# Four edits in a fused Mamba and mixture-of-experts kernel: the pieces of the first weight load, an undivided last block, further rows finished a block later, and the order of the gate's sums

## The chip, the cores and the metric

The kernel runs on one core of a Trainium2 chip. The metric is the device time of one execution in microseconds (us). The kernel before took 487.88 us, the median of three runs (486.55 to 489.39). One further execution was recorded by the hardware profiler; every duration below is from it.

A core has several engines that run their own instruction streams in order and wait for one another through semaphores. PE (TensorE) multiplies matrices and writes to PSUM banks; PEld is its loading of the stationary operand. DVE (VectorE), ACT (ScalarE) and POOL (GpSimd) work on tiles in SBUF and PSUM. SP (SyncE) mainly issues DMA transfers; POOL issues the indirect ones, which gather or scatter rows by a list of indices.

## The reference, cut to what matters

`x` holds 4096 tokens of width 256. A Mamba layer (inner width 512, 16 states, a convolution over 4 tokens) and a mixture of 8 experts (hidden width 1024, one expert for each token) follow each other, each with a residual sum and a layernorm. In short:

```python
xz = x @ W_in                                   # 256 -> 2 x 512
conv_in, gated = xz[..., :512], xz[..., 512:]
convolved = silu(depthwise_conv(conv_in, conv_w, 4 taps) + conv_b)
x_dbl = convolved @ W_x                         # delta, B (16), C (16)
delta = softplus(x_dbl[..., :1])
h_t = exp(delta * A) * h_(t-1) + delta * B * convolved[..., :16]
ssm_out = sum(h_t * C)                          # one number for each token
gated_out = (ssm_out + convolved * D_param) * silu(gated)
x1 = layernorm(x + gated_out @ W_out)
e = argmax(x1 @ Wr.T + br)                      # one expert for each token
out = layernorm(x1 + relu(x1 @ W1[e].T + b1[e]) @ W2[e].T + b2[e])
```

## The kernel before

**The Mamba layer** runs over 8 blocks of 512 tokens. The loop over k holds several blocks at once: block k is projected, block k-1 is gauged (`W_x`) and scanned, block k-2 passes the gate and the output projection, block k-3 is ranked for its experts. The channels lie on the 128 partitions, so the inner width of 512 is four column groups c = 0 to 3.

- `project` (L740 to L773) makes the products of `W_in` (L755), eight groups of 128 columns for each block: four for the convolution, four for the gate. Each needs two passes, since the 256 input columns are two times 128. In block 0 the first group alone is split into two halves of the tokens. ACT evicts each group (L760, L762, L764), and DVE adds the convolution's other three terms in `taps` (L736), which the text calls taps.
- `gauge` (L788), `scan` and `gate` (L868 to L885) follow. In the gate two products of TensorE, `py` at L873, write the state's sum for the first 256 tokens to one PSUM bank and for the second 256 to another. DVE then makes eight sums (L880): four column groups times two halves. The products with silu(gated) follow at L885, one for each group: those of groups 0, 1 and 2 on POOL, that of group 3 on DVE; in the last two blocks group 1 is on DVE too.
- `project_out` (L921 to L945) multiplies `sg`, the products' tile, by `W_out`: four steps j of 128 tokens, each over the four groups. It adds the residual, takes the layernorm's statistics and writes `x1` to memory (`x1d`). `choose` (from L948), `rank` (L975 to L1009) and `place` (L1020) work out each token's expert and place in the experts' lists; `table` and its `lookup` turn the counts into index tiles (`tidx` for rows, `widx` for weights).

**The experts** run as 32 blocks b of 128 rows, each with one expert's weights, in `blocks` (from L694). A block is cut into four quarters, which the main loop lays between the last Mamba blocks and runs in a row at the end:

- `prefetch` issues, up to two blocks ahead and on POOL, the gather of the rows (`xg`, L502) and that of the expert's weights (`we`, L520, three buffers).
- `scatter` (L661 to L663) writes the block before to `out`, on POOL.
- `turn` (L549, L551, L560) transposes the rows (`pg`), `hidden` makes the hidden layer: products at L577, the relu of the first half on ACT (L586), of the second on DVE (L588), both to `hT`.
- `close` (L590 to L645) multiplies `hT` by the second weights (L628) into the bank `pe`; `add_rows` makes the residual plus bias (L605). `finish` (L647 to L659) adds both to `r` (L650) and makes the layernorm (L251 to L262) with the result `y`.

Blocks 17, 20, 23, 26 and 29 (`LONG`) carry 32 or 64 **further rows** of the same expert besides their 128 (`ROOM`). Their products at L639 go to a bank `pf` of their own, and `finish` adds the bias to them (L656), sums the bank's parts (L658), makes a second layernorm and `scatter` a second DMA for them. All their tiles are slices of one buffer, called `long` in the trace. Block 31, the last, closes in two halves of the 256 output columns (L612): each half has eight products, its sum `r` (L621) and its statistics, so that the first half's sum can be made during the second half's products.

**What sets the order.** TensorE's instructions run in the order in which the program gives them (`manual_schedule` for PE alone). The order on DVE, ACT, POOL and SP is made by the planner of the tile framework, which may place an instruction elsewhere than its line stands. A bank (`ps.tile`, by tags `mm`, `tr` and `o`) or a buffer is handed on when its last reader is done.

**The start.** The loads are issued on two queues. SP loads the first half of each half of xT and `W_in` in pieces (`columns`), ACT loads the rest of xT:

```python
    for at in (slice(0, first), slice(first, TB)):
        nc.sync.dma_start(st[0]["xTb"][:, 0, at], xT[0:P, at])
        nc.scalar.dma_start(st[0]["xTb"][:, 1, at], xT[P : 2 * P, at])
        columns(slice(0, P) if at.start == 0 else slice(P, DI))
```

So `W_in` comes in pieces of 128, 384 and 512 columns, the first behind the first half of the tokens, the second behind the second half. The small loads `cw` and `cb` follow on ACT, and `wr` and the next blocks' loads on SP.

Of the kernel before, what the change touches and what calls it, by code (L numbers as in the profile page):

```python
# [37 lines left out]
F32 = mybir.dt.float32  # L38
# [61 lines left out]
def mamba_moe(  # L100
# [60 lines left out]
    for at in (slice(0, first), slice(first, TB)):  # L161
        nc.sync.dma_start(st[0]["xTb"][:, 0, at], xT[0:P, at])
        nc.scalar.dma_start(st[0]["xTb"][:, 1, at], xT[P : 2 * P, at])
        columns(slice(0, P) if at.start == 0 else slice(P, DI))
    cw = const.tile([P, CC, KC], F32, name="cw")
    nc.scalar.dma_start(cw, conv_w.rearrange("(c p) k -> p c k", p=P))
    cb = const.tile([P, CC], F32, name="cb")
# [80 lines left out]
        allow_small_or_imprecise_dtypes=True,  # L248
    )

    def layernorm(pool, rows, done, name, st=None):  # L251

        n = rows.shape[0]
        if st is None:
            st = pool.tile([P, 6], F32, tag="st", name=f"st{name}")[0:n, :]
            nc.vector.bn_stats(st, rows)
        mv = pool.tile([P, 2], F32, tag="mv", name=f"mv{name}")[0:n, :]
        nc.vector.bn_aggr(mv, st)  # L258
        sd = pool.tile([P, 1], F32, tag="sd", name=f"sd{name}")[0:n, :]
        nc.scalar.activation(sd, mv[:, 1:2], AF.Sqrt, bias=eps[0:n, :])  # L260
        nc.vector.reciprocal(sd, sd)
        nc.vector.tensor_scalar(done, rows, mv[:, 0:1], sd, ALU.subtract, ALU.mult)  # L262
# [232 lines left out]
    xgs, wes, turned, hid, last, open_, ys = {}, {}, {}, {}, {}, {}, {}  # L495


    xgf, openf, yf, ends_, wide_, xss, seldom_in, halves = {}, {}, {}, {}, {}, {}, [], []
    current = 0

    def gather(to, rows, at):
# [24 lines left out]
    def more_of(b):  # L526
        return ROOM[LONG[b]] if b in LONG else 0
# [64 lines left out]
    def close(b, half):  # L592
        we, hT = wes[b], hid[b]
        if half == 0:
            open_[b] = bank("o", f"pe{b}")
        py = open_[b]

        def out_weights(fc):
            return we[:, O2 + fc * D : O2 + (fc + 1) * D]

        def add_rows():
            xss[b] = m2.tile([P, D], F32, tag="xs", name=f"xs{b}")

            with tc.issue_after(last[b].ins):
                nc.vector.tensor_tensor(xss[b], xgs[b], we[:, OC : OC + D], ALU.add)  # L605

        if b == SURE - 1:


            at = slice(half * D // 2, (half + 1) * D // 2)  # L610
            for fc in range(FC):
                nc.tensor.matmul(  # L612
                    py[:, at], lhsT=hT[:, fc, :], rhs=out_weights(fc)[:, at],
                    start=(fc == 0), stop=(fc == FC - 1),
                )
            if half == 0:
                add_rows()
                halves.append(m2.tile([P, D], F32, tag="r", name=f"r{b}"))
                halves.append(a2.tile([P, 2, 6], F32, tag="sta", name=f"st{b}"))
            r, sts = halves  # L620
            nc.vector.tensor_tensor(r[:, at], py[:, at], xss[b][:, at], ALU.add)  # L621
            nc.vector.bn_stats(sts[:, half, :], r[:, at])
            if half == 1:
                ys[b] = m2.tile([P, D], F32, tag="y", name=f"y{b}")
                layernorm(m2, r, ys[b], f"m{b}", sts)
            return
        for fc in range(half * FC // 2, (half + 1) * FC // 2):
            nc.tensor.matmul(  # L628
                py[:, 0:D], lhsT=hT[:, fc, 0:P], rhs=out_weights(fc),
                start=(fc == 0), stop=(fc == FC - 1),  # L630
            )
        if half == 0:
            return
        if b in LONG:

            openf[b], n = bank("o", f"pf{b}"), more_of(b)
            for fc in range(FC):
                g = fc * n % P
                nc.tensor.matmul(  # L639
                    openf[b][g : g + n, 0:D], lhsT=hT[:, fc, P:], rhs=out_weights(fc),  # L640
                    start=(fc < P // n), stop=(fc >= FC - P // n), tile_position=(0, g),
                )
        add_rows()
        if b != SELDOM:
            finish(b)  # L645

    def finish(b):  # L647
        we, py, xs = wes[b], open_[b], xss[b]
        r = m2.tile([P, D], F32, tag="r", name=f"r{b}")
        nc.vector.tensor_tensor(r, py[:, 0:D], xs, ALU.add)  # L650
        ys[b] = m2.tile([P, D], F32, tag="y", name=f"y{b}")
        layernorm(m2, r, ys[b], f"m{b}")
        if b in LONG:
            m = more_of(b)
            xs, r, yf[b] = (ends_[b][0:m, n * D : (n + 1) * D] for n in (1, 2, 3))
            nc.vector.tensor_tensor(xs, xgf[b], we[0:m, OC : OC + D], ALU.add)  # L656
            for g in range(0, P, m):
                nc.vector.tensor_tensor(r, openf[b][g : g + m, 0:D], r if g else xs, ALU.add)  # L658
            layernorm(m2, r, yf[b], f"f{b}")  # L659

    def scatter(b):  # L661
        for rows, at in ((ys[b], index[b][1]), *(((yf[b], further[b][0 : more_of(b), :]),) if b in LONG else ())):
            moved = nc.gpsimd.indirect_dma_start(  # L663
                out=out, out_offset=bass.IndirectOffsetOnAxis(ap=at, axis=0),
                in_=rows, in_offset=None, bounds_check=T - 1, oob_is_err=False,
            )

            tc.declare_no_dep(moved.ins, group="rows", reason="blocks have no row in common")
            tc.add_to_no_dep_group("rows", moved.ins)
# [23 lines left out]
    def blocks():  # L693

        nonlocal current
        for b in range(SURE):
            current = b
            if b - 1 == SELDOM:
                seldom()
                finish(SELDOM)  # L700
            prefetch(b)

            if SELDOM - 6 <= b < SELDOM - 2:
                for n in range(SURE + b - SELDOM + 6, NSB, 4):
                    gather(seldom_rows()[:, (n - SURE) * D : (n - SURE + 1) * D], *index[n])

            if 0 < b:
                scatter(b - 1)
            for n in range(b + 2, NSB, 2) if b >= SURE - 2 else ():
                ys[n] = seldom_rows()[:, (n - SURE) * D : (n - SURE + 1) * D]  # L710
                scatter(n)
            if b not in turned:
                turn(b)
            hidden(b, 0)
            yield
            hidden(b, 1)
            yield
            if b + 1 in xgs and b + 1 < SURE:
                turn(b + 1)
            close(b, 0)  # L720
            yield
            close(b, 1)
            yield
# [9 lines left out]
    def taps(i, c):  # L733
        acc, xc = st[i]["acc", c], st[i]["xc"]
        for k in range(KC - 1):
            nc.vector.scalar_tensor_tensor(  # L736
                acc, xc[:, c, k : k + TB], cw[:, c, k : k + 1], acc, ALU.mult, ALU.add
            )

    def project(i, c):  # L740

        s = st[i]
# [5 lines left out]
            s["cv"] = a3.tile([P, CC, TB], F32, tag="cv", name=f"cv{i}")  # L748
            s["sg"] = a3.tile([P, CC, TB], F32, tag="sg", name=f"sg{i}")
        xc, cv, sg = s["xc"], s["cv"], s["sg"]  # L750
        pm = bank("mm", f"pm{i}_{c}")

        for at in (slice(0, first), slice(first, TB)) if i == c == 0 else (slice(0, TB),):
            for dc in range(DC):
                nc.tensor.matmul(  # L755
                    pm[:, at], lhsT=win[:, dc, c * P : (c + 1) * P], rhs=xTb[:, dc, at],
                    start=(dc == 0), stop=(dc == DC - 1),
                )
        if c >= CC:
            evicted = nc.scalar.activation(sg[:, c - CC, :], pm, AF.Silu)  # L760
        else:
            nc.scalar.copy(xc[:, c, KC - 1 :], pm)  # L762
            acc = a3.tile([P, TB], F32, tag="acc", name=f"acc{i}_{c}")
            evicted = nc.scalar.activation(  # L764
                acc, pm, AF.Identity, scale=cw[:, c, KC - 1 : KC], bias=cb[:, c : c + 1]
            )
            s["acc", c] = acc
            if c < CC - 1:
                taps(i, c)
# [96 lines left out]
    def gate(i):  # L866
        cv, sg = st[i]["cv"], st[i]["sg"]


        pys = [bank("o", f"py{i}_{g}") for g in range(2)]  # L870
        for g, py in enumerate(pys):
            at = slice(g * Q, g * Q + NS)
            nc.tensor.matmul(  # L873
                py[:, 0 : TB // 2], lhsT=ones[at, :], rhs=st[i]["hC"][at, :], start=True,
                stop=True, tile_position=(g * Q, 0),
            )
        for c in range(CC):
            for g, py in enumerate(pys):
                at = slice(g * TB // 2, (g + 1) * TB // 2)
                nc.vector.scalar_tensor_tensor(  # L880
                    cv[:, c, at], cv[:, c, at], dp[:, c : c + 1], py[:, 0 : TB // 2],
                    ALU.mult, ALU.add,
                )
            eng = nc.vector if c == CC - 1 or (c % 2 and i >= NB - 2) else nc.gpsimd
            eng.tensor_tensor(sg[:, c, :], cv[:, c, :], sg[:, c, :], ALU.mult)  # L885

# [321 lines left out]
```

## Time and profile before

| | |
|---|---|
| median of three runs | 487.88 us (486.55 to 489.39) |
| profiled execution | 486.12 us |
| its span, first to last instruction | 484.4 us |
| mean granted TensorE clock | 0.996 of full speed |
| moved by DMA | 89.65 MB, 185 GB/s |

The busy time of the engines in six stretches of the span shows where the work lies:

| us | stage | PE | DVE | ACT | POOL | GB/s |
|---|---|---|---|---|---|---|
| 0 to 10 | loads, first products | 8.1 | 1.3 | 2.8 | 3.3 | 219 |
| 10 to 40 | first two Mamba blocks | 29.3 | 19.3 | 23.9 | 0.7 | 88 |
| 40 to 170 | Mamba | 129.4 | 116.5 | 102.1 | 49.0 | 106 |
| 170 to 250 | Mamba and experts mixed | 79.2 | 66.8 | 47.5 | 31.7 | 158 |
| 250 to 400 | experts | 150.0 | 97.2 | 33.9 | 63.0 | 278 |
| 400 to 484.4 | experts, end | 75.3 | 39.3 | 13.8 | 38.2 | 197 |

How such lines are read. A busy-share line gives an engine, its busy us, the share of the span and the number of instructions. In a line of the waits the waiting engine, tile and line stand left of the arrow and the one that ended the wait right of it; then come the us in all, the number of waits and the mean. In a timeline a line has start, duration, engine, source line, operation, the tile written and the tiles read, and the shapes; "x16" says that so many like instructions are put together, and square brackets give the engine's idle time before and what ended it. Tile names leave out the block's number, and `pm`, `py`, `po`, `ph`, `pe`, `pf`, `pg` and `prx` are PSUM banks.

### The profile page before, as it was taken

To read this page: it belongs to the slowest core of one execution; us is meant where nothing else is said; L and a number is where in the kernel's file an instruction comes from. 1 tells how busy PE (TensorE), PEld (TensorE's weight loads), DVE (VectorE), ACT (ScalarE), POOL (GpSimd) and SP (SyncE) were. 2 spreads that over 40 slices of the span, in tenths; PEclk is the share of its full clock that TensorE was granted. 3 is DMA by queue.
4 is the path that set the end of the run, shared out by engine and by line. 5 is a ranking of instruction groups with operands and counts; after the bars stand their busy time and mean duration, and the time that the engine had idled before them with its cause. 6 is when DMAs were issued, how large, how long until landed. Compare 5 with 4: busy or idle time off the path is not lost. (4 is left out here: it accounts for less than half of the span.)

```text
span 484.4 us, 7580 instructions
## 1 busy us (share of the span) xinstructions
PE 471.3 (97%) x2618; PEld 352.9 (73%) x2618; DVE 340.3 (70%) x1117; ACT 224.0 (46%) x453; POOL 185.9 (38%) x194
## 2 busy tenths in 40 slices
PE   8999999999999999999999999999999999999984
PEld 5444555546464676777898999999989898889874
DVE  2587969798998997877799779445464645555343
ACT  3777768878878865848443132212111112122111
POOL 2001212444437454241514332535344456644621
PEclk9999999999999999999999999999999999999998
DMA  7501012130407918414677767999874399769700
GB/s 226 171 2 45 0 45 87 43 88 0 132 1 295 391 42 283 158 50 175 184 271 269 278 215 267 387 354 343 344 281 162 87 350 283 229 219 336 275 16 22
DMA packets 23049, 89.65 MB, mean 185 GB/s; under 512 B 4898, under 2 KB 14629, under 8 KB 19298
## 3 DMA queue, kind: packets, MB, share of 16 engines
q0 software_dynamic: 8672, 74.38, 42.2%
q1 hardware_dynamic: 13378, 14.50, 9.5%
q8 instruction: 21, 0.34, 0.3%
q10 hardware_dynamic: 960, 0.27, 0.3%
q14 instruction: 18, 0.15, 0.1%
HBM read 87.45 MB, written 9.54 MB: 200 GB/s over the span
## 5 line engine op out<-in xcount | busy, mean ns | idle before, releaser
L755 PE MATMUL pm<-xTb,win 128*128 128x512 f32 (+1 forms) x260 | 121.3, 597 | 0.2 <-DMA win<-in_W_in 0.2
L577 PEld LDWEIGHTS ph<-xgT,we 128*128 128x128 f32 x864 | 100.9, 192 | 6.3 <-issue 2.8
L577 PE MATMUL ph<-xgT,we 128*128 128x128 f32 x864 | 103.4, 276 | 0.6 <-issue 0.6
L628 PE MATMUL pe<-we,hT 128*128 128x256 f32 x416 | 96.1, 381 | 1.4 <-ACT hT L586 1.0
L628 PEld LDWEIGHTS pe<-we,hT 128*128 128x128 f32 x416 | 76.7, 190 | 11.9 <-ACT hT L586 1.2
L736 DVE SCALAR_TENSOR_TENSOR acc<-xc,cw,acc 128x512 f32<-128x512 f32 x96 | 72.9, 780 | 16.0 <-ACT acc L764 15.6
L755 PEld LDWEIGHTS pm<-xTb,win 128*128 128x128 f32 x260 | 47.6, 192 | 47.0 <-issue 40.9
L260 ACT ACTIVATE sdm<-mvm,eps 128x1 f32<-128x1 f32 x32 | 9.5, 296 | 143.7 <-DVE mvm L258 118.7
L520 POOL DMA_INDIRECT we<-in_experts,widx x32 | 33.7, 1054 | 90.5 <-DVE r L650 25.3
L921 PE MATMUL po<-wout,sg 128*128 128x264 f32 x256 | 64.1, 392 | 0.0
L885 POOL TENSOR_TENSOR sg<-cv,sg 128x512 f32<-128x512 f32 x22 | 32.8, 1495 | 59.3 <-DVE cv L880 45.9
L921 PEld LDWEIGHTS po<-wout,sg 128*128 128x128 f32 x256 | 46.1, 190 | 10.1 <-issue 2.9
L663 POOL DMA_INDIRECT out<-y,tidx x32 | 32.8, 1024 | 35.8 <-DVE y L262 23.4
L588 DVE TENSOR_SCALAR hT<-ph,we 128x128 f32<-128x128 f32 x108 | 31.4, 342 | 20.3 <-issue 8.8
L650 DVE TENSOR_TENSOR r<-pe,xs 128x256 f32<-128x256 f32 x31 | 13.1, 422 | 44.2 <-PE pe L628 37.7
L502 POOL DMA_INDIRECT xg<-x1d,tidx x32 | 32.1, 1004 | 31.0 <-DVE xd L811 7.5
L586 ACT ACTIVATE hT<-ph,we 128x128 f32<-128x128 f32 x108 | 30.7, 367 | 21.1 <-PE ph L577 14.3
L1009 POOL TENSOR_SCALAR rowh<-lrow,row,code 128x256 f16<-128x256 bf16 x20 | 26.0, 1308 | 27.2 <-DVE row L1001 26.0
L880 DVE SCALAR_TENSOR_TENSOR cv<-cv,dp,py 128x256 f32<-128x256 f32 x64 | 28.6, 471 | 3.4 <-PE py L873 3.4
L760 ACT ACTIVATE sg<-pm 128x512 f32<-128x512 f32 x32 | 19.0, 595 | 18.4 <-PE pm L755 16.0
L762 ACT COPY xc<-pm 128x512 f32<-128x512 f32 x32 | 18.6, 582 | 18.0 <-PE pm L755 17.8
L764 ACT ACTIVATE acc<-pm,cb,cw 128x512 f32<-128x512 f32 x32 | 25.1, 784 | 0.0
(224 smaller groups left out, 619.4 us busy)
## 6 DMA issues: line engine op xcount, KB each, us to landing
xb<-in_x SPq DMA_DIRECT2D x8, 512.0 KB, 6.2
x1d<-x SPq DMA_DIRECT2D x8, 512.0 KB, 6.0
xTb<-in_xT SPq DMA_DIRECT2D x7, 512.0 KB, 6.1
win<-in_W_in SPq DMA_DIRECT2D x1, 512.0 KB
we<-in_W_outT SPq DMA_DIRECT2D x1, 512.0 KB
wout<-in_W_out SPq DMA_DIRECT2D x1, 512.0 KB
we<-in_experts,widx POOLq DMA_INDIRECT x32
xg<-x1d,tidx POOLq DMA_INDIRECT x32
```

The costliest lines, as they stand in the source:

```text
L502: nc.gpsimd.indirect_dma_start(out=to, out_offset=None, in_=x1d[0:rows, :], in_offset=bass.IndirectOffsetOnAxis(ap=at, axis=0),)
L520: nc.gpsimd.indirect_dma_start(out=wes[n][:, :], out_offset=None, in_=experts, in_offset=bass.IndirectOffsetOnAxis(ap=weights[n], axis=0), ...
L577: nc.tensor.matmul(ph[:, n * w : (n + 1) * w], lhsT=we[:, at : at + P], rhs=xgT[:, dc * w : (dc + 1) * w], start=(dc == 0), stop=(dc == DC ...
L586: nc.scalar.activation(hT[:, fc, :], ph[:, n * w : (n + 1) * w], AF.Relu, bias=bias)
L588: last[b] = nc.vector.tensor_scalar(hT[:, fc, :], ph[:, n * w : (n + 1) * w], bias, 0.0, ALU.add, ALU.max)
L628: nc.tensor.matmul(py[:, 0:D], lhsT=hT[:, fc, 0:P], rhs=out_weights(fc), start=(fc == 0), stop=(fc == FC - 1),)
L663: moved = nc.gpsimd.indirect_dma_start(out=out, out_offset=bass.IndirectOffsetOnAxis(ap=at, axis=0), in_=rows, in_offset=None, bounds_chec ...
L736: nc.vector.scalar_tensor_tensor(acc, xc[:, c, k : k + TB], cw[:, c, k : k + 1], acc, ALU.mult, ALU.add)
L755: nc.tensor.matmul(pm[:, at], lhsT=win[:, dc, c * P : (c + 1) * P], rhs=xTb[:, dc, at], start=(dc == 0), stop=(dc == DC - 1),)
L880: nc.vector.scalar_tensor_tensor(cv[:, c, at], cv[:, c, at], dp[:, c : c + 1], py[:, 0 : TB // 2], ALU.mult, ALU.add,)
L885: eng.tensor_tensor(sg[:, c, :], cv[:, c, :], sg[:, c, :], ALU.mult)
L921: nc.tensor.matmul(po[:, 0 : D + NE], lhsT=sg[:, c, j * P : (j + 1) * P], rhs=wout[:, c, :], start=(c == 0), stop=(c == CC - 1),)
```

## The change

Four edits are made at once.

1. **First loads and products.** `W_in` comes in pieces of 128, 128, 256 and 512 columns; the second piece stands in front of the second half of xT. In block 0 the first two column groups are both split into halves of the tokens: TensorE makes group 0's first half, group 1's first half, group 0's second, group 1's second.
2. **The last block.** Block 31 closes like every other: eight products over all 256 columns, one sum, one set of statistics. `layernorm` loses its argument for statistics made before.
3. **Further rows.** Their bias is added in `close`; the bank's sums and the layernorm move into `finish_further`, which is called a block later, behind `hidden(b, 1)`. Their scatter comes a block later too, behind that of the next block's rows.
4. **The gate.** The sums of the first half (bank 0) are made for all four groups ahead of those of the second half, except for group 0, whose second sum stays second. The product of a group follows its second sum.

```diff
-        columns(slice(0, P) if at.start == 0 else slice(P, DI))
+        if at.start == 0:
+            columns(slice(0, P))
+            columns(slice(P, 2 * P))
+    columns(slice(2 * P, DI))
...
-    def layernorm(pool, rows, done, name, st=None):
+    def layernorm(pool, rows, done, name):
         n = rows.shape[0]
-        if st is None:
-            st = pool.tile([P, 6], F32, tag="st", name=f"st{name}")[0:n, :]
-            nc.vector.bn_stats(st, rows)
+        st = pool.tile([P, 6], F32, tag="st", name=f"st{name}")[0:n, :]
+        nc.vector.bn_stats(st, rows)
...
-        if b == SURE - 1:
-            at = slice(half * D // 2, (half + 1) * D // 2)
-            for fc in range(FC):
-                nc.tensor.matmul(
-                    py[:, at], lhsT=hT[:, fc, :], rhs=out_weights(fc)[:, at],
...
-            if half == 1:
-                ys[b] = m2.tile([P, D], F32, tag="y", name=f"y{b}")
-                layernorm(m2, r, ys[b], f"m{b}", sts)
-            return
...
-        add_rows()
+        xss[b] = m2.tile([P, D], F32, tag="xs", name=f"xs{b}")
+        with tc.issue_after(last[b].ins):
+            nc.vector.tensor_tensor(xss[b], xgs[b], we[:, OC : OC + D], ALU.add)
+        if b in LONG:
+            nc.vector.tensor_tensor(
+                ends_[b][0 : more_of(b), D : 2 * D], xgf[b], we[0 : more_of(b), OC : OC + D],
+                ALU.add,
+            )
         if b != SELDOM:
             finish(b)
...
+    def finish_further(b):
         if b in LONG:
             m = more_of(b)
             xs, r, yf[b] = (ends_[b][0:m, n * D : (n + 1) * D] for n in (1, 2, 3))
-            nc.vector.tensor_tensor(xs, xgf[b], we[0:m, OC : OC + D], ALU.add)
             for g in range(0, P, m):
                 nc.vector.tensor_tensor(r, openf[b][g : g + m, 0:D], r if g else xs, ALU.add)
             layernorm(m2, r, yf[b], f"f{b}")
...
             if 0 < b:
                 scatter(b - 1)
+                scatter(b - 2, False)
...
             hidden(b, 1)
+            finish_further(b - 1)
             yield
...
+        if i == 0 and c < 2:
+            if c == 0:
+                for n in range(2):
+                    products(n, slice(0, first))
+            products(c, slice(first, TB))
+        else:
+            products(c, slice(0, TB))
...
+        def skip(c, g):
+            at = slice(g * TB // 2, (g + 1) * TB // 2)
+            nc.vector.scalar_tensor_tensor(
+                cv[:, c, at], cv[:, c, at], dp[:, c : c + 1], pys[g][:, 0 : TB // 2],
+                ALU.mult, ALU.add,
+            )
+        skip(0, 0)
+        skip(0, 1)
+        for c in range(1, CC):
+            skip(c, 0)
         for c in range(CC):
-            for g, py in enumerate(pys):
-                at = slice(g * TB // 2, (g + 1) * TB // 2)
-                nc.vector.scalar_tensor_tensor(
-                    cv[:, c, at], cv[:, c, at], dp[:, c : c + 1], py[:, 0 : TB // 2],
-                    ALU.mult, ALU.add,
-                )
+            if c:
+                skip(c, 1)
             eng = nc.vector if c == CC - 1 or (c % 2 and i >= NB - 2) else nc.gpsimd
             eng.tensor_tensor(sg[:, c, :], cv[:, c, :], sg[:, c, :], ALU.mult)
```

More of the change, by code (lines that the diff above doesn't have):

```diff
@@ L495, in mamba_moe @@
     xgs, wes, turned, hid, last, open_, ys = {}, {}, {}, {}, {}, {}, {}
-    xgf, openf, yf, ends_, wide_, xss, seldom_in, halves = {}, {}, {}, {}, {}, {}, [], []
+    xgf, openf, yf, ends_, wide_, xss, seldom_in = {}, {}, {}, {}, {}, {}, []
     current = 0
@@ L599, in out_weights @@
             return we[:, O2 + fc * D : O2 + (fc + 1) * D]
[L601 to L605, printed above, removed]
-        if b == SURE - 1:
-            at = slice(half * D // 2, (half + 1) * D // 2)
-            for fc in range(FC):
-                nc.tensor.matmul(
-                    py[:, at], lhsT=hT[:, fc, :], rhs=out_weights(fc)[:, at],
-                    start=(fc == 0), stop=(fc == FC - 1),
-                )
-            if half == 0:
-                add_rows()
[L618 to L622, printed above, removed]
-            if half == 1:
-                ys[b] = m2.tile([P, D], F32, tag="y", name=f"y{b}")
-                layernorm(m2, r, ys[b], f"m{b}", sts)
-            return
         for fc in range(half * FC // 2, (half + 1) * FC // 2):
@@ L642, in close @@
                 )
-        add_rows()
+        xss[b] = m2.tile([P, D], F32, tag="xs", name=f"xs{b}")
[6 more added lines that the diff above has]
+            )
         if b != SELDOM:
@@ L659, in finish, with scatter @@
             layernorm(m2, r, yf[b], f"f{b}")
-    def scatter(b):
-        for rows, at in ((ys[b], index[b][1]), *(((yf[b], further[b][0 : more_of(b), :]),) if b in LONG else ())):
+    def scatter(b, main=True):
+        rows_at = ((ys[b], index[b][1]),) if main else ()
+        if not main and b in LONG:
+            rows_at = ((yf[b], further[b][0 : more_of(b), :]),)
+        for rows, at in rows_at:
             moved = nc.gpsimd.indirect_dma_start(
@@ L738, in taps @@
             )
+    banks = {}
     def project(i, c):
@@ L750, in project, with products @@
         xc, cv, sg = s["xc"], s["cv"], s["sg"]
-        pm = bank("mm", f"pm{i}_{c}")
-        for at in (slice(0, first), slice(first, TB)) if i == c == 0 else (slice(0, TB),):
+        def products(c, at):
+            if c not in banks:
+                banks[c] = bank("mm", f"pm{i}_{c}")
             for dc in range(DC):
                 nc.tensor.matmul(
-                    pm[:, at], lhsT=win[:, dc, c * P : (c + 1) * P], rhs=xTb[:, dc, at],
+                    banks[c][:, at], lhsT=win[:, dc, c * P : (c + 1) * P], rhs=xTb[:, dc, at],
                     start=(dc == 0), stop=(dc == DC - 1),
                 )
+        if i == 0 and c < 2:
[5 more added lines that the diff above has]
+            products(c, slice(0, TB))
+        pm = banks.pop(c)
         if c >= CC:
@@ L876, in gate @@
             )
-        for c in range(CC):
-            for g, py in enumerate(pys):
-                at = slice(g * TB // 2, (g + 1) * TB // 2)
-                nc.vector.scalar_tensor_tensor(
-                    cv[:, c, at], cv[:, c, at], dp[:, c : c + 1], py[:, 0 : TB // 2],
-                    ALU.mult, ALU.add,
-                )
+        def skip(c, g):
[8 more added lines that the diff above has]
+            skip(c, 0)
+        for c in range(CC):
+            if c:
+                skip(c, 1)
             eng = nc.vector if c == CC - 1 or (c % 2 and i >= NB - 2) else nc.gpsimd
```

## The prediction

> **What bounds the kernel now.** I read the page's busy shares first, then the table of TensorE's waits, then the stretches in order of time around the four edits.
>
> ```profile
> PE 471.3 (97%) x2618; PEld 352.9 (73%) x2618; DVE 340.3 (70%) x1117; ACT 224.0 (46%) x453; POOL 185.9 (38%) x194
> ```
>
> TensorE works from start to end. Its waits show how little could be won back:
>
> ```profile
> PE pe L628 <- ACT hT L586: 1.0, 1, 1.0
> ...
> PE pg L549 <- DMA xg<-x1d,tidx: 0.6, 1, 0.6
> ...
> PE prx L894 <- DVE rk L994: 0.4, 1, 0.4
> ...
> PE pe L612 <- DVE r L621: 0.4, 1, 0.4
> ```
>
> Apart from the time before the first product, no wait of TensorE is over 1.0 us, and none names a weight load, a bank held by the gate's sums, or the further rows' scatter. So an edit gains only where it takes away one of these few waits or shortens the two ends, and it loses wherever it makes one of TensorE's operands late. The tightest such operand is in the gate. This is the timeline in the gate of block 2 (start, duration, engine, line, tile; in brackets the idle time before it and what ended it):
>
> ```profile
> 102.25 0.47 DVE L880 SCALAR_TENSOR_TENSOR cv<-cv,dp,py 128x256 f32<-128x256 f32 x1
> ...
> 102.81 1.92 POOL L885 TENSOR_TENSOR sg<-cv,sg 128x512 f32<-128x512 f32 x1 [1.28 <-DVE cv L880]
> ...
> 104.54 2.23 PE L921 MATMUL po<-wout,sg 128*128 128x264 f32 x8
> 104.67 0.74 DVE L736 SCALAR_TENSOR_TENSOR acc<-xc,cw,acc 128x512 f32<-128x512 f32 x1
> 105.33 0.68 DVE L885 TENSOR_TENSOR sg<-cv,sg 128x512 f32<-128x512 f32 x1
> ...
> 106.06 0.30 PEld L921 LDWEIGHTS po<-wout,sg 128*128 128x128 f32 x2 [0.44 <-DVE sg L885]
> ```
>
> The output projection starts at 104.54 while the products of the gate are still being made: POOL's last ends at 104.73, DVE's at 106.01, and TensorE waits for the latter. Its eight passes are 0.22 apart, two for each of the four column groups, so the groups are wanted at 104.54, 104.98, 105.43 and 105.87.
>
> **The change part by part.** Edits without effect first. In the order in which the changed program issues its instructions, DVE and ACT take the **further rows** exactly where they did, in front of the next block's hT; the planner puts them back. Only four of the five further scatters move on POOL's queue, behind the next block's xg and weight gathers and its y (the fifth, of block 29, stays). Those gathers are issued some 0.9 us (one scatter) earlier, plus what POOL waited for the rows (6.7 us in three waits); TensorE waits for no weights, so this is 0, and a weight gather is never later. The **earlier release of the first PSUM bank** is 0 as well: no wait on it stands in the table. Both are hidden by slack that was there before.
>
> **The tail.** Now the last block closes in two column halves:
>
> ```profile
> 476.33 2.05 PE L612 MATMUL pe<-we,hT 128*128 128x128 f32 x16 [0.38 <-DVE r L621]
> ...
> 478.42 0.29 DVE L621 TENSOR_TENSOR r<-pe,xs 128x128 f32<-128x128 f32 x1 [1.81 <-PE pe L612]
> ...
> 479.85 0.41 DVE L262 TENSOR_SCALAR y<-r,mvm,sdm 128x256 f32<-128x256 f32 x1
> ```
>
> Products start at 474.00, y ends at 480.26: 6.26 us. The form it takes instead stands in block 30: products at 466.87, sum r at 470.63 (3.76 us), y ends at 472.70 (2.07 us more), together 5.83. The wider add and statistics (0.42 and 0.43 against 0.29 each) cost less than the wait between the halves, so **-0.43**; bounds 0 and -0.7.
>
> **The start.** The loads of W_in put a second 128-column piece in front of the second half of xT.
>
> ```profile
> 4.57 1.35 PEld L755 LDWEIGHTS pm<-xTb,win 128*128 128x128 f32 x4 [0.52 <-issue]
> 6.66 0.73 PEld L755 LDWEIGHTS pm<-xTb,win 128*128 128x128 f32 x4 [0.73 <-DMA xTb<-in_xT]
> 7.75 0.30 PEld L755 LDWEIGHTS pm<-xTb,win 128*128 128x128 f32 x2 [0.37 <-DMA win<-in_W_in]
> ```
>
> The first piece is unchanged, so products start at 4.57 and the first half ends at about 6.4. I take the new piece to land where the xT half did, 6.66; the second group's first half runs to 7.63. The xT half lands 128 KB later, at the 226 GB/s of the page's first slice 0.58 us, so about 7.24: in time. Two second halves of 0.86 bring the third group to 9.35, against 9.58 now (7.75 with four passes of 0.43 and a slow first one): **-0.2**. Bounds -0.35 (all idle gone) and +0.4 (xT as late as 8.2). SP's queue has one issue more (0.4 to 0.5 us) ahead of wr, the next xT and the rest; the router product that needs wr comes at 10.9, the others after 17. The first eviction moves from 7.82 to about 8.6, and with it DVE's taps; the cover is 4.6 us (block 0's last cv ends at 20.02, is read at 24.62).
>
> **The gate.** Here the edit costs. Of eight sums L880 two finish a column group. Before, group 1 was complete after the 4th sum, group 2 after the 6th, group 3 after the 8th; now all first halves come first, so groups 1, 2, 3 are complete after the 6th, 7th and 8th. The slots between the taps stay. POOL's product for group 1 thus moves from 99.70 to where that for group 2 was, and group 2's has to follow it directly. Do POOL and DVE disturb each other? The same form takes POOL 1.27 us beside sums and 1.92 beside a tap; and in the gate of block 1, where three products run back to back from 71.08 to 74.85, a tap took
>
> ```profile
> 73.59 1.81 DVE L736 SCALAR_TENSOR_TENSOR acc<-xc,cw,acc 128x512 f32<-128x512 f32 x1
> ```
>
> instead of 0.74. [...] Taken without it, 1.27 us for each product, group 2 would come in time and the gate would cost 0; with it: no product runs at 99.70, so DVE's L965 (0.78 there, 0.18 at 75.81) is free, and the 6th sum ends 0.60 earlier, at 102.12. Product 1 takes its row's 1.92: 102.21 to 104.13. Product 2 follows with 1.27: to 105.40, just as TensorE wants it. But the tap that ran free at 104.67 is now issued at 104.07 and held; as at 73.59 the next instruction follows 1.73 later (75.32), at 105.80, and that is product 3: to 106.48, with 0.05 for the signal 106.53, wanted at 105.87. TensorE loses 0.66 and 0.11 for a slow restart, 0.77 in place of today's 0.30 (0.19 and 0.11): **+0.5**.
>
> Gate of block 3 has the same times within 0.1: +0.5. It is followed by the wait for rk above (at 138.7), which could absorb that; but DVE runs gapless from 128 to 140 and is itself 0.47 later, so the wait ends later too and I absorb nothing. Gate of block 4: product 3 ends at 160.21 instead of 159.74, wanted at 160.05, loss 0.3; then DVE's lateness moves tidx (163.70), behind it POOL's gather of xg, and the wait of pg for xg ends 0.47 later: +0.5 for the pair. In the gates of blocks 0, 1, 5, 6 and 7 the last product comes ahead of its use by 1.6, 0.9, 7, 5 and 2 us; a hold of up to 1.2 us fits, save for a little in block 1. Sum of the gates **+1.5**; bounds +0.3 (waits after gates 3 and 4 absorb, the hold half as long) and +4.2 (1.4 each: product 2 starved behind tap and product 3, and DVE 1.3 late afterwards).
>
> **Sum.** +1.5 - 0.43 - 0.2 = +0.9 us. The profiled execution took 486.12 (span 484.4 and 1.7 around it), so 487.0; the runs' median is 487.88, 1.76 above it, and the same step gives **488.8**.
>
> **The rivals.**
>
> - *The gates pile up (slower).* Place: gates of blocks 2 to 4. If POOL's second product is passed over by the tap and by product 3 (0.66 + 0.61), group 2 comes at 106.7, a net loss of 1.13, and DVE is 1.27 late where rank and gather are waited for: 1.13 + 1.27 + 1.27 = 3.7, less 0.63: 491.0 or more. For: POOL's 1.92 shows that it can lose its turn. Against: at 72.31 and 73.58 it got it each time. It decides from 1.02 us lost per gate (3.07 together is 2.44 after the gains).
> - *The further rows' stall goes (faster).* In block 30 TensorE idles about 2.1 us, since
>
> ```profile
> 464.69 0.88 DVE L658 TENSOR_TENSOR long<-pf,long 64x256 f32<-64x256 f32 x2 [3.58 <-remote]
> ...
> 466.87 3.72 PE L628 MATMUL pe<-we,hT 128*128 128x256 f32 x16 [0.97 <-ACT hT L586]
> ```
>
>   hT stands on ACT behind the further rows' square root. Finishing them later would take that away: -2.1 - 0.63, without a gate loss 485.2. Against: the issue order of DVE and ACT has not changed there, so in this part the change doesn't do what it says.
> - *The gates are hidden (nothing but the ends).* The operands slip inside slack, -0.63: 487.25.
>
> **How the numbers follow.** Likeliest case 0.66 (486.8 to 490.2 by its bounds and the runs' own spread of 1.4 each way), pile-up 0.12, stall gone 0.06, hidden 0.16. 0.5% is 2.44 us, about what a measurement of this kernel can tell from no change: the lines are 485.4 and 490.3. Slower: the pile-up and a little of the likeliest case's upper end, 0.13. Faster: most of the stall's case, 0.05. Within: 0.82. The range 486.7 to 491.0 leaves out the stall case and the far ends.
>
> **What the profile after would show.** Start: three L755 weight loads' waits at 6.66 and 7.75 gone or under 0.2, third group near 9.35. Gates 2 to 4: POOL's three L885 as one early and two adjoining, a tap of 1.7 to 1.8 after them, the wait of po's load for sg at 0.8 to 0.9 instead of 0.44. Tail: 5.8 us from the last block's first product to the end of y. Wrong would be: a wait of TensorE on POOL's sg over 1 us, a wait on win over 0.5, or sdf behind hT on ACT.

## The result, and the profile after

The changed kernel takes **495.39 us** (median of four, 493.37 to 496.49) where the kernel before takes 488.29 beside it (486.55 to 489.39): a ratio of 1.0143, 95% interval 1.0100 to 1.0186, or 7.1 us slower. The forecast was 488.8 with a range up to 491.0. The profiled execution of the changed kernel took 494.83 us (span 493.1), 8.7 us above the profiled one of before.

When this was measured both kernels ran slower than in any later set: before alone stood at 488 there and at 483.9 to 484.6 in four later sets, in whose 187 executions it never passed 486.81; in three of those sets the change was measured again, and came out 0.9 to 1.7 us slower.

Where do the 8.7 us lie? Like instructions of TensorE were put beside each other in the two traces. They are 1.8 us late when block 0's router products begin (18.78 against 16.98), 5.0 late behind the gates of blocks 2 to 4 (183.93 against 178.91), 9.3 late in block 30 (474.84 against 465.51), and 8.7 at the end. So: start +1.8, gates +3.2, expert blocks +4.3, tail -0.6.

First the page's busy shares, then the waits of TensorE in the profile after (waiting engine and line, what ended the wait; us in all, number, and the longest single wait, not the mean as was said where the views were explained):

```profile
PE 475.4 (96%) x2606; PEld 355.0 (72%) x2606; DVE 344.3 (70%) x1115; ACT 223.5 (45%) x453; POOL 185.3 (38%) x194
```

```profile
PE pe L604 <- ACT hT L588: 3.2, 2, 2.3
PE po L933 <- DVE sg L897: 1.7, 3, 0.6
...
PE pm L749 <- DMA win<-in_W_in: 0.6, 1, 0.6
...
PE po L933 <- POOL sg L897: 0.6, 2, 0.3
```

All four are new or larger: `po` now waits for the gate's products in five places, the first products wait for `W_in`, and one wait for hT is 2.3 us long.

**The start** (timeline after, TensorE and its weight loads):

```profile
4.44 2.04 PE L749 MATMUL pm<-xTb,win 128*128 128x256 f32 x4
7.06 6.19 PE L749 MATMUL pm<-xTb,win 128*128 128x256 f32 x16 [0.58 <-DMA win<-in_W_in]
```

```profile
7.06 4.50 PEld L749 LDWEIGHTS pm<-xTb,win 128*128 128x128 f32 x14 [1.30 <-DMA win<-in_W_in]
```

The second piece lands at 7.06, 0.4 us later than I took it to. But this is the smaller part of the cost: the fourteen loads behind it take 4.50 us, and the passes of 256 columns follow each other by 0.43 us until 10.2, where before they had gone over to 0.22 by 7.0. TensorE stays at half rate.

**The gate of block 2** (timeline after, chosen lines of DVE, POOL and PEld):

```profile
103.39 0.47 DVE L883 SCALAR_TENSOR_TENSOR cv<-cv,dp,py 128x256 f32<-128x256 f32 x1
103.88 0.73 DVE L728 SCALAR_TENSOR_TENSOR acc<-xc,cw,acc 128x512 f32<-128x512 f32 x1
103.94 1.83 POOL L897 TENSOR_TENSOR sg<-cv,sg 128x512 f32<-128x512 f32 x1 [3.10 <-DVE cv L883]
104.54 1.28 DVE L981 TENSOR_TENSOR oh<-back,best 128x32 bf16<-128x32 f32 x1
105.74 0.47 DVE L883 SCALAR_TENSOR_TENSOR cv<-cv,dp,py 128x256 f32<-128x256 f32 x1
106.29 1.27 POOL L897 TENSOR_TENSOR sg<-cv,sg 128x512 f32<-128x512 f32 x1 [0.52 <-DVE cv L883]
106.64 0.94 DVE L984 TENSOR_TENSOR earlier<-earlier,here 128x8 bf16<-128x8 bf16 x1
107.61 0.30 PEld L933 LDWEIGHTS po<-wout,sg 128*128 128x128 f32 x2 [0.70 <-POOL sg L897]
108.17 0.68 DVE L897 TENSOR_TENSOR sg<-cv,sg 128x512 f32<-128x512 f32 x1
108.90 0.30 PEld L933 LDWEIGHTS po<-wout,sg 128*128 128x128 f32 x2 [0.99 <-DVE sg L897]
```

POOL's product for group 1 stands where the forecast put it (103.94 is 102.21 in the time of before, since all is 1.73 late here). What it holds is not a tap but `oh`, a small one-hot operation: 1.28 us, where before it took 0.18, although POOL's product for group 2 was running there (102.81, 1.92 us, shown in the prediction):

```profile
103.40 0.18 DVE L969 TENSOR_TENSOR oh<-back,best 128x32 bf16<-128x32 f32 x1
```

The seventh sum, queued behind it, starts 7.86 us after `py` instead of 7.35, group 2's product waits for that sum, and TensorE waits for both remaining products. Group 2's product in turn stands beside `earlier`, another small two-input operation (0.94 here, 0.34 before), and behind that in DVE's queue come a tap and the product for group 3.

**Block 25** (timeline after, then TensorE's granted clock in three stretches: start and end, length, busy us and instructions of PE, clock, DMA share, GB/s):

```profile
426.44 1.14 ACT L588 ACTIVATE hT<-ph,we 128x128 f32<-128x128 f32 x4 [4.44 <-remote]
426.56 1.13 DVE L590 TENSOR_SCALAR hT<-ph,we 128x128 f32<-128x128 f32 x4 [3.91 <-remote]
```

```profile
423.40:426.80 3.40, 1.12 (x8) 1.00 0.90 160
426.80:430.20 3.40, 3.33 (x8) 0.50 0.18 58
430.20:433.60 3.40, 3.40 (x20) 1.00 0.08 25
```

TensorE has finished the hidden layer's products at 423.8, but ACT and DVE, which wait for them alone, go on only at 426.4; "remote" means that the profile finds no releaser. TensorE stands for 2.3 us, and its next 3.4 us run at half rate: 2.3 and half of 3.4 make the 4.05 lost here. The trace of before has such a wait, of 3.58 us in block 30, which the forecast took for a stall of the kernel's own. The trace of after has it too, at the same place, beside the one in block 25:

```profile
473.92 0.88 DVE L644 TENSOR_TENSOR long<-pf,long 64x256 f32<-64x256 f32 x2 [3.62 <-remote]
```

In both traces TensorE stands in block 30 for 0.4 and 0.2 us with nothing named and then for 0.9 to 1.0 us for hT. None of the fourteen profiles taken later, of any kernel, has these waits.

**The tail**:

```profile
483.23 3.62 PE L604 MATMUL pe<-we,hT 128*128 128x256 f32 x16
...
486.88 0.42 DVE L635 TENSOR_TENSOR r<-pe,xs 128x256 f32<-128x256 f32 x1 [2.00 <-PE pe L604]
...
488.55 0.41 DVE L264 TENSOR_SCALAR y<-r,mvm,sdm 128x256 f32<-128x256 f32 x1
```

From the last block's first product to the end of y: 5.73 us, where it was 6.26.

### The profile page after: what moved, and what is told of

Same layout as the page of the kernel before. It is cut to its first block, busy times and chain, and to the rows that moved or that the text cites. A ratio compares the mean times of both kernels' runs of the same rounds, so it can differ in the third digit from the quotient of the medians.

```text
span 493.1 us, 7553 instructions
## 1 busy us (share of the span) xinstructions
PE 475.4 (96%) x2606; PEld 355.0 (72%) x2606; DVE 344.3 (70%) x1115; ACT 223.5 (45%) x453; POOL 185.3 (38%) x194
## 5 line engine op out<-in xcount | busy, mean ns | idle before, releaser
L749 PE MATMUL pm<-xTb,win 128*128 128x512 f32 (+1 forms) x264 | 122.7, 598 | 0.6 <-DMA win<-in_W_in 0.6
L604 PE MATMUL pe<-we,hT 128*128 128x256 f32 x432 | 101.2, 386 | 3.2 <-ACT hT L588 3.2
L604 PEld LDWEIGHTS pe<-we,hT 128*128 128x128 f32 x432 | 80.8, 193 | 14.5 <-ACT hT L588 3.6
L728 DVE SCALAR_TENSOR_TENSOR acc<-xc,cw,acc 128x512 f32<-128x512 f32 x96 | 71.7, 769 | 17.2 <-ACT acc L768 16.9
L749 PEld LDWEIGHTS pm<-xTb,win 128*128 128x128 f32 x264 | 49.6, 196 | 46.8 <-issue 39.8
L579 PE MATMUL ph<-wide,we 128*128 128x160 f32 (+1 forms) x160 | 24.6, 311 | 1.1 <-DVE r L635 0.7
```

The lines of the kernel that those rows point to most:

```text
L579: nc.tensor.matmul(ph[:, n * w : (n + 1) * w], lhsT=we[:, at : at + P], rhs=xgT[:, dc * w : (dc + 1) * w], start=(dc == 0), stop=(dc == DC ...
L604: nc.tensor.matmul(py[:, 0:D], lhsT=hT[:, fc, 0:P], rhs=out_weights(fc), start=(fc == 0), stop=(fc == FC - 1),)
L728: nc.vector.scalar_tensor_tensor(acc, xc[:, c, k : k + TB], cw[:, c, k : k + 1], acc, ALU.mult, ALU.add)
L749: nc.tensor.matmul(banks[c][:, at], lhsT=win[:, dc, c * P : (c + 1) * P], rhs=xTb[:, dc, at], start=(dc == 0), stop=(dc == DC - 1),)
```

## The experiments

Changes in us are the ratio's distance from 1 times the 484 us of before.

**Each edit alone.** Four kernels, each before with one edit.

The start: the loads and the order of the first products, as in the change's diff.

> Before with the first edit alone (four pieces of W_in, two split column groups). The clock theory: TensorE waits about 0.8 us for the second piece near 6.3 us, that wait keeps it at half rate until about 10.2 us, and the router product pw starts 1.8 us later than before (13.1 instead of 11.3): time +1.8 us, about 489.8. The rival, that the wait alone costs: full rate again from about 8 us, pw at most 0.6 us later, +0.6. A third, that the profiled execution was an accident of its loads: -0.2 to 0.

Measured: 482.74 against 484.29, ratio 0.9974 (0.9956 to 0.9991), -1.3 us. The clock theory's +1.8 did not come; nor did a loss of any size.

```profile
6.71 4.57 PE L760 MATMUL pm<-xTb,win 128*128 128x256 f32 x16 [0.26 <-DMA win<-in_W_in]
11.12 0.51 PE L474 MATMUL pw<-wr,ones 128*128 128x8 f32 x4
```

Here the piece lands at 6.71, the sixteen passes take 4.57 us instead of 6.19, and `pw` begins at 11.12. So the loss of 1.8 us is not in every execution of this edit. Nor does this profile show where the whole gain comes from: `pw` is only 0.17 ahead of before's 11.29.

The gate:

> Before with the fourth edit alone (all first halves of the gate's sums ahead). If the profile of the change is typical, TensorE waits twice in each of the gates of blocks 2 and 3 (0.45 and 0.74 beyond a pass) and once in block 4's, blocks 2 to 4 add 1.1, 1.1 and 1.0 us, in all +3.2 us: about 491.2. The forecast's own size, one wait of 0.66 in each, would give +1.5: 489.5.

Measured: 486.67 against 484.29, ratio 1.0049 (1.0031 to 1.0068), +2.4 us. That interval, +1.5 to +3.3, holds the 3.2 of the first profile and touches the forecast's 1.5; the profile decides. Its three gates are those of the change to 0.01 us: +1.11, +1.10 and +0.96 at the marks behind them. They are the same within 0.02 us in all five profiles with the changed gate.

The further rows, run in two sets:

> Before with the third edit alone (further rows finished and scattered a block later). The forecast's step says 0: DVE and ACT keep their order, only four scatters move on POOL's queue; block 25 shows no wait of TensorE above 0.7 us: about 488. The rival, that the move on POOL's queue makes the 4 us loss seen in block 25 of the changed kernel: +4 us, about 492, with ACT and DVE both idle for about 4 us ahead of hT in block 25.

> The third edit alone once more, beside the changed kernel. If the large loss comes from the further rows' place on POOL's queue, then whenever the changed kernel loses over 4 us this one does too. If not, it stays within 0.5 us of before. In both cases blocks 17, 20, 23 and 26 keep the order of DVE and ACT, and only POOL's scatter moves.

Measured: ratio 1.0004 (0.9990 to 1.0018) and 0.9996 (0.9981 to 1.0010). No wait on "remote" is in either profile. The forecast's 0 holds, to within the 0.9 us of the intervals.

The tail:

> Before with the second edit alone (last block undivided). The forecast's step says -0.43: 5.8 us from the last block's first product to the end of y, about 487.6. The rival, that the single block costs more than it saves (its sum has to wait for all products): 0 or up to +0.5.

Measured: 483.35 against 484.29, ratio 0.9988 (0.9969 to 1.0007), -0.6 us, and 5.73 us from the first product to the end of y. The interval holds 0 as well; the trace's -0.53 is the better number: the stretch is 5.73 in all six profiles with the undivided block, and 6.25 or 6.26 in all ten with the divided one.

**The change again**, three times, beside other kernels.

> The changed kernel as it is, once more. If the four edits add up as each did alone (-1.3, +2.4, +0.2, -0.6), it is 0.7 us slower than before; in the profile gates of blocks 2 to 4 as in the first profile (+3.2), and no 4 us loss in block 25. The rival, that the edits act together or that the loss in block 25 is theirs: 5 to 9 us slower again, with ACT and DVE idle for 4 us ahead of hT in block 25.

> The changed kernel a third time. By the sum of the single edits and its second measurement it is 1 to 2.5 us slower than before. The rival: where the first measurement's conditions return (before near 488, above the 484 of the later runs), it is 5 to 9 us slower, and the profile shows a loss of 2 us or more in one of the blocks 24 to 30, with DVE waiting for nothing that the program names.

> The changed kernel once more, for the loss in block 25 alone. If before stands near 484 again, the changed kernel is 1 to 2.5 us slower and shows no such loss; if before stands near 488, as in the first measurement, it should be 5 to 9 us slower and show a loss of 2 us or more in blocks 24 to 30. Anything else (before near 484 and the change over 4 us slower, or before near 488 and the change within 2.5) would tie the loss to the change or free it from it.

Measured: 485.25, 485.18 and 485.15; ratios 1.0036 (1.0018 to 1.0053), 1.0028 (1.0015 to 1.0042) and 1.0019 (1.0005 to 1.0033): +1.7, +1.4 and +0.9 us. The sum of the single edits is -1.3 + 2.4 + 0.2 - 0.6 = +0.7, a little under all three; each of its terms is itself uncertain by 0.7 to 0.9. The loss in block 25 is in none of these profiles, and before was near 484 each time: the first measurement's conditions did not come back, so whether that loss needs them and the change together is not told. The second profile shows the start with a wait as long as in the first:

```profile
6.93 2.89 PEld L749 LDWEIGHTS pm<-xTb,win 128*128 128x128 f32 x14 [1.27 <-DMA win<-in_W_in]
```

The same fourteen loads behind the same wait (1.27 and 1.30) take 2.89 us here and took 4.50. Between these two profiles the wait does not decide, the clock does: here the full rate had begun at 5.65, ahead of the wait.

**The start's wait made longer, and filled.** The late piece:

```diff
-        if at.start == 0:
-            columns(slice(0, P))
-            columns(slice(P, 2 * P))
+        columns(slice(0, P) if at.start == 0 else slice(P, 2 * P))
     columns(slice(2 * P, DI))
```

> The first edit alone, with its second piece of W_in moved back behind the second half of xT, so that TensorE always waits for it, about 1 us near 6.3. The clock theory: a wait of that length keeps the clock at half rate for another 3.4 us, to about 10.2; pw at 12.8 to 13.3 instead of 11.1, time +1.5 to +2 against before. The rival, that only the wait counts: full rate before 8 us, pw at 11.6, time +0.3.

Measured: 484.51 against 483.87, ratio 1.0000 (0.9982 to 1.0017); the medians' difference of 0.6 us lies within that interval. The edit missed its aim: in the profile the piece still lands at about 6.4, TensorE does not wait and `pw` stands at 10.96. So the clock theory of the start was not tested here. This profile loses 1.6 us elsewhere, at 44 us, which is read in the last section.

With the wait filled:

```diff
-                for n in range(2):
-                    products(n, slice(0, first))
+                products(0, slice(0, first))
+                for n in range(5):
+                    nc.tensor.transpose(idle[:, n % 4 * P : (n % 4 + 1) * P], ident, ident)
+                products(1, slice(0, first))
```

> As the one with the late piece, but five transposes of the identity (0.21 us each at half rate, results unused) fill TensorE's wait for that piece. The clock theory: the clock goes up as in the kernel before, by about 7 us, and pw stands at 11.3 to 11.7, 1 to 2 us earlier than with the empty wait, although TensorE has more to do and the same loads to wait for. The rival: the same time as the late piece without the transposes, or later by part of their 1.07 us.

Measured: 483.20, ratio 0.9978 (0.9966 to 0.9990), -1.1 us, though TensorE has more to do. One of its 20 executions lies above 484.2 us; of the late piece's 12 it is 8, all eight at a granted clock of 0.995 where the other four have 0.996 to 0.999. But `pw` at 11.36 is later than without the transposes, so the reason given in the expectation is not shown: since the late piece made no wait, this pair does not tell whether the transposes help at the start or by what comes later. This profile also shows something about the gate, which is before's own here. In block 2 TensorE waits 0.96 us for the product of group 3, because `oh` is held in the old order too:

```profile
103.47 1.30 DVE L985 TENSOR_TENSOR oh<-back,best 128x32 bf16<-128x32 f32 x1
```

**What in the gate costs.** The edit alone, with POOL's product for group 1 left out:

```diff
-            eng.tensor_tensor(sg[:, c, :], cv[:, c, :], sg[:, c, :], ALU.mult)
+            if c != 1 or i >= NB - 2:
+                eng.tensor_tensor(sg[:, c, :], cv[:, c, :], sg[:, c, :], ALU.mult)
```

> The fourth edit alone, and in the gates of blocks 0 to 5 POOL's product for column group 1 is left out (that group's sg stays silu(gated); outputs and the experts' lists differ, so only the gates of blocks 2 to 4 are read, not the whole time). The theory that POOL's product 1 holds DVE: the small one-hot operation that took 1.28 us there takes about 0.2, the seventh sum comes 1.1 us earlier than with the edit alone, TensorE's waits for sg in gates 2 and 3 shrink from 1.2 us to 0.2 at most. The rival, that the sums' new order alone makes the products late: the seventh sum within 0.3 us of its place with the edit alone, and waits of at least 0.5.

```profile
102.94 0.18 DVE L978 TENSOR_TENSOR oh<-back,best 128x32 bf16<-128x32 f32 x1
103.05 0.47 DVE L879 SCALAR_TENSOR_TENSOR cv<-cv,dp,py 128x256 f32<-128x256 f32 x1
...
103.60 1.27 POOL L894 TENSOR_TENSOR sg<-cv,sg 128x512 f32<-128x512 f32 x1 [4.35 <-DVE cv L879]
...
106.21 0.30 PEld L930 LDWEIGHTS po<-wout,sg 128*128 128x128 f32 x2 [0.45 <-DVE sg L894]
```

`oh` is back at 0.18, the seventh sum starts 6.75 us after `py` (7.86 with the edit, 7.35 before), the last wait is 0.45, and was 0.44 before. In the three gates TensorE loses nothing against before, although `earlier` is still held (0.94 or 0.95). With that product left out the new order of the sums is free; the product that meets `oh` is the cost.

The same product on DVE, nothing left out:

```diff
-            eng = nc.vector if c == CC - 1 or (c % 2 and i >= NB - 2) else nc.gpsimd
+            eng = nc.vector if c % 2 else nc.gpsimd
```

> The fourth edit alone, with the product of column group 1 on DVE instead of POOL in every block (nothing is left out). The theory that POOL's product 1 holds DVE's one-hot operation: that operation falls from 1.28 to about 0.2 us, DVE takes 0.68 for the product instead, so its queue is 0.4 us ahead of the edit alone, and TensorE's waits in gates 2 to 4 fall from 3.2 us in all to 1 to 2.2; time +1 to +2 against before. The rival, that the new order of the sums costs by itself: no less than the edit alone, +2.4 or more.

Measured: 485.35 against 484.56, ratio 1.0022 (1.0007 to 1.0036), +1.1 us. `oh` takes 0.18. But DVE now has 0.68 more to do in each gate, and TensorE waits once for a product in each of gates 2 to 4 (0.60, 0.61 and 0.33 beyond a pass). Within the theory's +1 to +2; the rival's +2.4 lies outside the interval.

**Parts put together.** The change without its gate:

> The change without its fourth edit: first loads, undivided last block and further rows as changed, gate as before. Sum of the single results: -1.3 -0.6 +0.2 = -1.7 us against before, and no wait above 0.2 us of TensorE for sg in the gates of blocks 2 to 4. The rival, that the gate is not what costs: slower than before still.

Measured: 483.65 against 484.47, ratio 0.9983 (0.9970 to 0.9996), -0.8 us. The sign is as expected, and with the gate in the same set the change is at 485.18: the gate costs 1.5 net there. Half the expected gain is missing; the last section shows where this profile loses it.

The first edit with three transposes in the wait, and the undivided last block; gate and further rows as before:

> A version put together from the parts: the first edit with three transposes of the identity (0.64 us at half rate) in TensorE's wait for the second piece, and the undivided last block, gate and further rows as before. The parts' sum: start -1.1 to -1.3, tail -0.6, together -1.7 to -1.9 us, with few executions in the group 2 us above the fastest. The rival, that the transposes delay the start by their own length when the piece comes early: -0.6 to -1.1.

Measured: **482.68** against 484.47, ratio 0.9970 (0.9959 to 0.9982), -1.4 us, between the parts' sum and the rival's -0.6 to -1.1; the interval, -0.9 to -2.0, reaches into both. It has the lowest median of these kernels; before and the change (485.18) ran in the same set, but the first edit alone, at 0.9974 in another, is not clearly slower.

## Why the prediction was wrong

In the first profile the prediction's sum of +0.9 met +8.7: -0.2 for the start met +1.8, +1.5 for the gates +3.2, 0 for the expert blocks +4.3, and -0.43 for the tail -0.6. The first two misses are explained below; the third and largest is not. Without it +4.4 would be left.

**The start** was the first step that failed: -0.2 forecast, +1.8 in the first profile. The piece was taken to land at 6.66 and landed at 7.06; that alone would be 0.4, and the wait of 0.58 for `win` is over the 0.5 that the prediction named as a sign of being wrong. The upper bound of +0.4 looked only at when data arrive, and not at the rate at which TensorE goes on behind the wait. The trace's record of the granted clock gives the rest. In the first profile of the change a full-rate stretch of 416.43 us, a half-rate one of 3.413 and a full-rate one of 61.44 follow each other: 122, 1 and 18 times 3.413. In the sixteen profiles the full-rate stretches last between 37.55 and 477.87 us, each a multiple of 3.413 (11 to 140 of them), and a half-rate one between two of them 3.41. So the changes of rate in these records lie whole steps of 3.41 us apart; such a step is called a window here. Ahead of the first full-rate stretch the record is empty, and the rate is read from the passes, 0.43 us apart. In thirteen of the sixteen profiles that stretch begins at 5.06 to 6.72 us, in two at 7.06 and 7.29. In the first profile of the change it begins at 10.37: one step earlier, at 6.96, the wait was about to end, TensorE had stood idle for 0.47 of the 3.41 us, and it ran at half rate for another window, worth 1.7 us. In the other fifteen profiles TensorE is idle for at most 0.17 us in the window that ends with the rise. In the second profile of the change the rise came at 5.65, ahead of the same wait; its 0.85 us then fell into a window at full rate, and the rate stayed. No experiment brought the loss back, so this account rests on the comparison of these profiles; that the idle time kept the rate down is the author's estimate from them. The forecast used both rates, some 0.43 for a pass of the first half and 0.22 for one of the "two second halves of 0.86", and did not ask what makes the one turn into the other.

**The gate** failed in one assumption: that the product for group 2 "has to follow it directly". The place was right, POOL's product 1 ran at 102.21 in before's time as forecast. That POOL and DVE hold each other up shows in three rows of before: 1.81 instead of 0.74 us for a tap at 73.59, 0.78 instead of 0.18 for L965 at 100.79, 1.92 instead of 1.27 for POOL at 102.81. In the profile after, product 1 took 1.83 instead of 1.27 beside a tap and ended at 105.77, and `oh`, issued beside it, took 1.28 instead of 0.18 and ended at 105.82. But the forecast let a tap at 104.67 be held and left the sums in their slots, and the profile after does not show that hold: this tap took its 0.74, at 107.50. In fact `oh`, 0.18 us long and thus overlooked, is the first two-input operation that DVE issues behind product 1. It is held for 1.1 us, and the seventh and eighth sums stand behind it, so product 2 starts 0.5 us after the end of product 1. The row that lent product 1 its 1.92 us was the warning: there `oh` had slipped in ahead of POOL. In blocks 2 to 4 of the nine profiles with before's gate it does so 26 times of 27 (`oh` 0.17 or 0.18, POOL's product 1.91 or 1.92); the one exception is the one shown above. In the five profiles with the changed gate it is held all 15 times (1.28 to 1.30, POOL's product 1.83 or 1.84). So in the gates of blocks 2 and 3 TensorE has a wait for POOL and one for DVE, in block 4 one for DVE: 1.1, 1.1 and 1.0 instead of 0.5 each, 3.2 instead of 1.5 in sum. That nothing would be absorbed by the later waits was right in sum: of block 4's 0.95, 0.39 is taken up in the wait for xg, and 0.5 is lost again when `xgT` comes late.

**The expert blocks** stood at 0 and lost 4.3 us more than before's, nearly all in block 25 (4.05). The kernel's order of instructions does not explain it, and no experiment reproduced it: the further rows alone are at 0 in two sets, and the change's three later profiles lack it. What held back the signals of products that by the trace ended at 422.0 and 423.8 until 426.4 stays open. So does what set the first measurement apart: the four later sets ran on four different chips, with only 0.7 us between their medians of before, but the chip of the first is not on record. The rival "the further rows' stall goes" named a 2.1 us stall of block 30 as the kernel's own, caused by the order of ACT behind a square root. It did not go in the first profile of the change, and it is absent from all fourteen later profiles, those with before's own order of further rows included. It was of the same kind as the wait in block 25, and the trace said so with the word "remote".

**What was right.** The tail: -0.43 forecast, -0.53 in the trace (its sum r and statistics as costed; the products' stretch was 3.65 to r instead of 3.76). The further rows' place on POOL's queue: 0. The earlier release of the bank: 0, since no wait on it has appeared or gone. In the three later measurements +0.9 to +1.7 stands against the forecast's +0.9, but that is luck: the gates cost about twice what was forecast in the traces, and the first edit, measured alone, gained 1.3 where -0.2 was forecast.

**The three rivals.** "The gates pile up" is nearest to what happened, with its price of about 1.1 a gate; it was given 0.12, and its mechanism was another one (POOL passed over). The gates were not hidden, and no stall went.

## What to carry to other kernels

Before a product on POOL is moved, look at every DVE instruction that will be issued beside it, the shortest too: here a small operation with two inputs was held until POOL's product ended (`oh`, 1.28 instead of 0.18 us), and with it whatever stood behind it in the queue. Price a wait of TensorE also by the rate at which TensorE goes on behind it: in the first profile of the change, at half rate, 0.47 us idle in a window of 3.41 went with another 1.7 lost, while in the second, at full rate, a wait of 0.85 us cost no more than itself. A wait with no releaser is no property of the kernel until a profile from another occasion has it; here two kernels measured on one occasion shared it, and no later profile did.

## What the runs showed of the hardware

Half-rate windows came in mid-kernel too, without a long wait. In four profiles (the late piece, the change's third, the second of the further rows, the change without its gate) TensorE ran one window of 3.41 us at half rate from about 44 us. This is the change's third profile, TensorE's timeline and its clock in three stretches:

```profile
41.49 0.95 PE L490 MATMUL pwo<-wr,we 128*128 128x8 f32 x8
42.63 1.15 PE L877 MATMUL py<-hC,ones 16*128 16x256 f32 x4 [0.19 <-DVE hC L865]
43.71 3.68 PE L749 MATMUL pm<-xTb,win 128*128 128x512 f32 x4
```

```profile
40.40:43.80 3.40, 3.21 (x16) 1.00 0.48 157
43.80:47.30 3.50, 3.50 (x4) 0.51 0.01 2
47.30:50.70 3.40, 3.40 (x13) 1.00 0.00 0
```

By the busy time TensorE was hardly idle (3.21 of 3.40 us), but from 41.49 on its products had 8 columns or 16 rows. The same four products took 1.98 us with the start edit alone. In the window ahead of that half rate, 1.36 us are products with 128 rows and 512 columns. The windows with the same instructions in two other traces, where full rate followed, have as much busy time and more of these products: in before the one from 40.48 to 43.89 is busy for 3.22 us, 1.89 of them such products, and in the first profile of the change the one from 44.50 to 47.92 for 3.22 us, 1.70 of them such products. So in these three windows the busy time does not tell which rate follows. That the products of 8 columns or 16 rows count for less is the author's estimate from them; no experiment varied it.

The window at 44 us also gives the missing part of the change without its gate: its first products were 0.77 us ahead of before's, and this window, 1.70 us, is what it lost after.
